# Late additions on VectorE, row copies one key step behind their norms, routing exponentials within slots as powers by GpSimd, and late weight fills spread

## The chip, the cores and the metric

The kernel runs on one core of a Trainium2 chip. The core has five engines with a queue each: TensorE (PE, with its weight loads shown as PEld), VectorE (DVE), ScalarE (ACT), GpSimd (POOL) and SyncE (SP), which here only issues transfers. Each engine takes its own instructions in order, and an instruction that waits holds everything behind it on that engine. The metric is the device time of one execution in microseconds (us), and less is better.

## The reference

Two layers, each an attention over a graph of 2708 nodes with 256 features, and then a mixture of eight experts with two experts for each node:

```python
# layer 0
x = x + elu(softmax(where(adj > 0, q @ k.T / 16, -9e15)) @ v)       # q, k, v of layernorm(x)
x = x + experts0(layernorm(x))      # layernorm again, router, top 2 of 8, gelu(xe @ W1 + b1) @ W2 + b2, hidden 1024
# layer 1
x = x + softmax(where(adj > 0, s_src + s_dst, -1e9)) @ H            # H = layernorm(x) @ W_fc
x = x + experts1(layernorm(x))      # softmax over 8, top 2 of 8, the same with hidden 512
```

The weight of a chosen expert is a softmax: in layer 0 over the two best router values, in layer 1 over all eight. Everything is float32; `adj` is int32.

## The kernel before

The 2708 rows are 22 tiles of 128 rows (the last has 20). Layer-0 attention goes over six blocks of queries (five of 512 and one of 148). A block goes over the 22 tiles of keys, one *key step* each: scores on TensorE, the exponential on ScalarE (L596), the mask on VectorE (L599), and, three key steps later, the product with the values (L648). The scores have two PSUM buffers, so TensorE can be at most two key steps ahead of ScalarE's exponential.

When a block is done, its result tiles are finished and *routed* beside the next block's key steps. This is a chain of small steps for each tile, written as Python generators (`finish`, then `route`). A class `Line` keeps the running chains; each `line.step()` moves every running chain to its next `yield`, oldest first, and starts a new one after every `gap` steps. In layer-0 attention there is one `line.step()` for a key step; in the expert stages there are two for a slot. A chain in layer 0 is: the ELU (L656 to L664), the addition of x (L669 or L671), statistics (L280 to L282), the power for the norm on GpSimd (L286), the normed row (L290), the second copy of the row on ScalarE (L1480), router values, the two best, the exponential on ScalarE (L1525), a count by matmul (L1528, L1529), the weights and the destination (L1531 to L1543), and two indirect transfers from GpSimd that scatter the row to its two experts (L1546). Tiles 0 to 15 get their router values by products on VectorE, tiles 16 to 21 by a transpose and a matmul. In layer 1 tiles 17 to 21 are still in the chain when the expert stage begins; they reach L1525 within it.

An expert stage goes over *slots*: 128 rows for one expert. A slot transposes the gathered rows (L1803), multiplies up (L1830), applies Gelu on ScalarE (L1838, after the scaled bias at L1823), multiplies down (L1846, one slot behind), weights the result on VectorE (L1852) and scatters it from GpSimd (L1868 in layer 0, L1858 in layer 1). GpSimd also fetches the weights of a later slot (L1736) and pads the experts' row lists (L1565), once the last tile is routed. SP fetches rows of later slots (L1755, L1761). The weights lie in a ring of SBUF buffers. In layer 1 the ring has eight buffers; four are filled before the stage (L1729), and four by ScalarE's own transfers in the first slots (L1881, `fill`), two in slot 0 and one each in slots 1 and 2.

The order of TensorE, ScalarE and VectorE is the order in which the program is written (`manual_schedule`), from block 1 of layer-0 attention on through the expert stage, and again in layer 1; SP's order is written out throughout. GpSimd's order in these stages is left to the framework's scheduler.

Of the kernel before, what the change touches and what calls it, by code (L numbers as in the profile page):

```python
# [9 lines left out]
F32 = mybir.dt.float32  # L10
# [5 lines left out]
AF = mybir.ActivationFunctionType  # L16
ALU = mybir.AluOpType
AX = mybir.AxisListType
PSUM = bass.MemoryType.PSUM

P = 128
# [3 lines left out]
E = 8  # L25
# [81 lines left out]
def adj_ffn_kernel(ctx: ExitStack, tc: tile.TileContext, a: dict, out: bass.AP):  # L107
    nc = tc.nc

    const = ctx.enter_context(tc.tile_pool(name="const", bufs=1))  # L110
# [13 lines left out]
    make_identity(nc, ident)  # L124
    minus_half = const.tile([P, 2], F32, name="minus_half")
    nc.gpsimd.memset(minus_half, -0.5)

    minus_big = const.tile([P, P], BF16, name="minus_big")
    nc.vector.tensor_scalar(minus_big, ident, -BIG, None, ALU.mult)
# [137 lines left out]
    def gate_dots(lg, x, r, experts, unused):  # L267

        for e in experts:
            nc.vector.scalar_tensor_tensor(  # L270
                unused, x, 1.0, wr_rows[:r, e],
                op0=ALU.mult, op1=ALU.mult, accum_out=lg[:r, e : e + 1],
            )
# [108 lines left out]
    def layer0_attention(line):  # L382
        with ExitStack() as scope, ExitStack() as until_last:
# [269 lines left out]
            def finish(t, raw, total):  # L653
                r, xr = ROWS[t], xin.pop(t)
                rinv = over_sum(raw, r, D, total, alone[:r, t : t + 1])
                nc.vector.scalar_tensor_tensor(  # L656
                    raw[:r, :D], raw[:r, :D], rinv, bv_b[:r], op0=ALU.mult, op1=ALU.add
                )
                neg = rows0.tile([P, D], F32, name="neg", bufs=2)
                nc.vector.tensor_scalar(neg[:r], raw[:r, :D], 0.0, None, ALU.min)  # L660
                yield
                nc.scalar.activation(neg[:r], neg[:r], AF.Exp)
                yield
                nc.vector.scalar_tensor_tensor(  # L664
                    neg[:r], neg[:r], -1.0, raw[:r, :D], op0=ALU.add, op1=ALU.max
                )
                x1 = rows0.tile([P, D], F32, name="x1")
                if t < experts0.early:
                    nc.vector.tensor_add(x1[:r], neg[:r], xr[:r])  # L669
                else:  # L670
                    nc.gpsimd.tensor_add(x1[:r], neg[:r], xr[:r])  # L671
                    yield
                yield from experts0.route(t, x1)

            def evict(b, accs, total):
# [12 lines left out]
            for b, (b0, nb, ts_) in enumerate(BLOCKS):  # L688
# [14 lines left out]
                for k in range(NT):  # L703
# [15 lines left out]
                    if len(late) > LAG:  # L719
                        b_, k_, p = late.pop(0)  # L720
# [410 lines left out]
    class Experts:  # L1131
        def __init__(self, layer, hidden, packed_weights, gate_bias, own_norm, xd, disp, early):
            self.hidden, self.packed_weights, self.own_norm = hidden, packed_weights, own_norm
            self.gate_bias, self.xd, self.disp = gate_bias, xd, disp

            self.seen = const.tile([P, E], BF16, name=f"seen{layer}")
            nc.vector.memset(self.seen, 0.0)
            self.routed, self.begun, self.pads = 0, False, []
            self.written = []
            self.groups = [f"written{layer}", f"late{layer}", f"apart{layer}", f"after{layer}", f"rows{layer}", f"summed{layer}"]  # L1140
            self.early = early
            self.side = "right" if own_norm else "left"


            n = FULL_AFTER[early]
            self.often = SURE + (2 if own_norm else 4)
            self.ring_size = RING if own_norm else E
            self.rows_ahead = ROWS_AHEAD if own_norm else ROWS_AHEAD + 1
            self.all_slots = SLOTS if own_norm else n + SLOTS
            self.then = {}  # L1150
            if not own_norm:
                self.sum_behind = self.often - E - 1
                return

            size = -(-(SURE - n) // RING)
            runs = [(0, 0, n // RING, 1), (n, size - 1, size, -1)]
            self.number = const.tile([P, SLOTS, 2], F32, name=f"number{layer}")
            number_i = const.tile([P, SLOTS], I32, name=f"number_i{layer}")
            for s0, c0, size, step in runs:
                nc.gpsimd.iota(  # L1160
                    number_i[:, s0 : s0 + size * RING], pattern=[[step, size], [size, RING]],
                    base=c0, channel_multiplier=0,
                )
            s0 = n + size * RING
            nc.gpsimd.iota(
                number_i[:, s0:], pattern=[[1, SLOTS - s0]], base=s0 - n, channel_multiplier=0
            )
            nc.vector.tensor_copy(self.number[:, :, 0], number_i)
            nc.vector.tensor_scalar(
                self.number[:, :, 1], self.number[:, :, 0], float(P), None, ALU.mult  # L1170
            )
# [266 lines left out]
        def route(self, t, x, logits=None):  # L1438


            own_norm, xd, disp, seen = self.own_norm, self.xd, self.disp, self.seen
            gate_bias = self.gate_bias
            r = ROWS[t]
# [4 lines left out]
            mean, once, twice, _ = norm_stats(x[:r], r)  # L1448
# [28 lines left out]
            if own_norm:  # L1477
                if by_dots:
                    gate_dots(dots, x[:r], r, range(E // 2, E), rows2[:r, 1, :D])
                nc.scalar.copy(rows2[:r, 1, :D], rows2[:r, 0, :D])  # L1480
            yield
            if not own_norm:
                (nc.vector.tensor_copy if self.begun else nc.scalar.copy)(
                    rows2[:r, 1, :D], rows2[:r, 0, :D]
# [25 lines left out]
            k = 2 if own_norm else E  # L1510
            p = small.tile([P, E], F32, name="p")
            den = small.tile([P, 2], F32, name="den")
# [9 lines left out]
                nc.vector.memset(sel, 0.0)  # L1522
            nc.vector.tensor_add(sel[:r], hot[:r, 0], hot[:r, 1])
            yield
            nc.scalar.activation(p[:r, :k], p[:r, :k], AF.Exp, accum_out=den[:r, 0:1])  # L1525
            yield
            ps = misc.tile([P, GROUP, P], F32, name="misc").rearrange("p g n -> p (g n)")
            nc.tensor.matmul(ps[:, :E], before, sel, start=True, stop=False)  # L1528
            nc.tensor.matmul(ps[:, :E], ones, seen, start=False, stop=True)  # L1529
# [263 lines left out]
        def slots(self, two, ps_mm, ps_acc, line):  # L1793
            hidden, own_norm, xd = self.hidden, self.own_norm, self.xd
# [82 lines left out]
            n = FULL_AFTER[self.early]  # L1877

            line.gap = 1 if own_norm else 2
            def fill(e):  # L1880
                nc.scalar.dma_start(  # L1881
                    self.ring[e], self.packed_weights[0][e * P : (e + 1) * P, :]
                )
# [4 lines left out]
            def slot(s, s1):  # L1888
                nonlocal placed, placing, behind, xe
                w, (_, who) = self.weights[s], self.rows_[s]  # L1890
                for _ in range(1 + (s == 0)):
                    if fills:
                        fill(fills.pop(0))
                after = turned(1) if s == 0 and not own_norm else None
                hT, bias2 = up(w, xe, who[:, 1:2])
                if s + 1 < s1:
                    xe = after or turned(s + 1)
                line.step()

                def fetch():  # L1900

                    for _ in range(2 if s + AHEAD < n else E):
                        if self.pads:
                            self.pads.pop(0)()
                    if len(self.weights) <= s + AHEAD < often:
                        self.weights.append(self.fetch_weights(s + AHEAD))
                    for _ in range(2):
                        at = len(self.rows_)
                        if at <= s + self.rows_ahead and at < (often if placed else n):
                            while at >= n and self.pads:  # L1910
                                self.pads.pop(0)()
                            self.rows_.append(self.fetch_rows(at))

                if own_norm and not placed and (not line.busy() or s + AHEAD == n):

                    line.finish()
                    for _ in self.place(n, SLOTS):
                        pass
                    placed = True
                if not own_norm and not placed and (not line.busy() or s + AHEAD == n):  # L1920
                    line.finish()
                    if placing is None:
                        placing = self.place_grid(n, self.all_slots)
                    for _ in range(2 if s + AHEAD < n else n):
                        if next(placing, self) is self:
                            placed = True
                            break
                if behind is None:
                    fetch()
                else:  # L1930
                    down(*behind, fetch)
                line.step()
                behind = (s, w, who, hT, bias2)
                if s % 2 == 1 and background:
                    background.pop(0)()
                for start in self.then.get(s, ()):
                    start()
# [177 lines left out]
```

## Time and profile before

| | us |
|---|---|
| median of three runs | 1181.54 |
| range of the runs | 1181.01 to 1186.1 |
| the profiled execution, own time | 1186.52 |
| its span, first to last instruction | 1184.7 |
| TensorE busy | 1134.8 |
| VectorE, ScalarE, GpSimd busy | 645.0, 431.0, 422.4 |
| mean granted TensorE clock | 0.979 |

The profile is of one execution, with times in us from the first instruction. The page gives busy time by engine, then the span in 40 slices; further views list the instructions in order of time (start, duration, engine, line, operation, output<-input, and in brackets how long the engine sat idle before and what ended that), groups of instructions by line and shape (count, busy time, mean in ns, idle before), and busy time with granted clock in chosen stretches. A "granted clock" under 1 means that TensorE was throttled for part of the stretch. Layer-0 attention lasts to about 495, the layer-0 experts to 816, layer-1 attention to 987, and the layer-1 experts to the end.

### The profile page before, as it was taken

How to read it: one execution, taken by the hardware profiler on the slowest of the kernel's cores; microseconds unless marked ns; L12 is line 12 of the kernel's file. 1: busy time of each engine (PE TensorE's matmuls, PEld its weight loads, DVE VectorE, ACT ScalarE, POOL GpSimd, SP SyncE). 2: the span in 40 equal slices, each digit the busy share in tenths (PEclk: the TensorE clock that was granted, in tenths of full speed). 3: DMA queues.
4: the chain of work that ended last, by engine and by line, in shares of the span. 5: the costliest groups of instructions: out<-in, count | busy, mean ns of one | idle time of the engine just before them, and what ended most of it. 6: DMA issues, size and time to landing. Idle time of an engine off the chain costs nothing. (4 is left out here: it accounts for less than half of the span.)

```text
span 1184.7 us, 20877 instructions
## 1 busy us (share of the span) xinstructions
PE 1134.8 (96%) x6421; PEld 919.7 (78%) x6421; DVE 645.0 (54%) x2391; ACT 431.0 (36%) x1258; POOL 422.4 (36%) x517
## 2 busy tenths in 40 slices
PE   8989999999999999899999999998999998999993
PEld 5666666666666675599999999997899997898993
DVE  5555687786887867544222222222876777732224
ACT  3222222222222222253333333332676664744441
POOL 3001212121212123244333343332663554665552
PEclk9999999999999999799999999999999998999997
DMA  9677775867855567548755955552200516577346
GB/s 219 130 163 189 187 183 143 241 165 186 224 129 163 140 154 302 178 125 292 197 155 154 325 128 138 162 161 58 63 1 28 210 51 207 148 241 237 79 119 239
DMA packets 198661, 195.88 MB, mean 165 GB/s; under 512 B 90939, under 2 KB 181524, under 8 KB 192520
## 3 DMA queue, kind: packets, MB, share of 16 engines
q1 hardware_dynamic: 173242, 118.18, 39.1%
q0 software_dynamic: 24256, 70.81, 18.8%
q10 hardware_dynamic: 1038, 5.40, 1.3%
q8 instruction: 55, 0.90, 0.3%
q14 instruction: 70, 0.57, 0.2%
HBM read 246.19 MB, written 66.15 MB: 264 GB/s over the span
## 5 line engine op out<-in xcount | busy, mean ns | idle before, releaser
L1830 PEld LDWEIGHTS mm<-xe,ring 128*128 128x128 f32 x2192 | 261.7, 194 | 9.6 <-ACT raw L678 1.8
L1830 PE MATMUL mm<-xe,ring 128*128 128x128 f32 x2192 | 263.9, 278 | 2.0 <-DVE xe L1803 1.0
L1846 PE MATMUL acc<-ring,hT 128*128 128x256 f32 x1096 | 253.8, 382 | 4.4 <-ACT hT L1838 4.4
L1838 ACT ACTIVATE hT<-mm,ring 128x128 f32<-128x128 f32 x548 | 155.7, 368 | 262.5 <-issue 151.0
L1846 PEld LDWEIGHTS acc<-ring,hT 128*128 128x128 f32 x1096 | 202.5, 191 | 29.1 <-ACT hT L1838 5.1
L648 PEld LDWEIGHTS acc<-v,p 128*128 128x128 f32 (+1 forms) x880 | 160.0, 190 | 62.4 <-issue 36.9
L648 PE MATMUL acc<-v,p 128*128 128x257 f32 (+1 forms) x880 | 202.7, 383 | 0.0
L584 PE MATMUL s<-g,xnT 128*128 128x512 f32 x420 | 201.2, 600 | 0.6 <-DVE mT L603 0.6
L1852 DVE SCALAR_TENSOR_TENSOR y<-acc,who,bias 128x256 f32<-128x256 f32 x92 | 44.4, 483 | 266.1 <-PE acc L1846 246.5
L1546 POOL DMA_INDIRECT disp<-row,to x88 | 91.2, 1037 | 270.6 <-DVE x L669 122.9
L286 POOL TENSOR_TENSOR ln_rs<-ln_rs,minus_half 128x2 f32<-128x2 f32 x88 | 68.8, 783 | 168.1 <-DVE ln_rs L282 126.3
L932 PE MATMUL acc<-parts,m 128*128 128x266 f32 x924 | 126.2, 293 | 0.0
L932 PEld LDWEIGHTS acc<-parts,m 128*128 128x128 f32 x924 | 117.0, 185 | 4.1 <-ACT raw L959 0.9
L1736 POOL DMA_INDIRECT ring<-L_ffn_packed,weight_row x76 | 80.2, 1055 | 111.9 <-PE acc L1846 76.3
L584 PEld LDWEIGHTS s<-g,xnT 128*128 128x128 f32 x420 | 77.2, 191 | 55.1 <-issue 49.5
L596 ACT ACTIVATE p<-s 128x512 f32<-128x512 f32 x105 | 62.3, 596 | 138.8 <-PE s L584 122.6
L599 DVE SCALAR_TENSOR_TENSOR p<-p,mT 128x512 f32<-128x512 f32 x100 | 70.9, 709 | 72.5 <-ACT p L596 72.4
L1868 POOL DMA_INDIRECT xd<-y,who x45 | 71.4, 1587 | 90.3 <-DVE xe L1809 47.3
L899 ACT CAST m<-mT 128x512 fp32r<-128x512 fp8e4 (+4 forms) x168 | 71.9, 475 | 9.6 <-PE acc L932 6.1
L1858 POOL DMA_INDIRECT xd<-y,who x47 | 49.6, 1055 | 51.1 <-DVE y L1852 42.1
L270 DVE SCALAR_TENSOR_TENSOR row<-x,wr_rows 128x256 f32<-128x256 f32 x128 | 54.4, 425 | 3.3
L1809 DVE TENSOR_SCALAR xe<-xe_raw,ring 128x128 f32<-128x128 f32 x90 | 27.3, 352 | 35.7 <-DMA ring<-L_ffn_packed,weight_row 33.7
(336 smaller groups left out, 1094.8 us busy)
## 6 DMA issues: line engine op xcount, KB each, us to landing
adj<-in_adj_dram SPq DMA_DIRECT2D x100, 256.0 KB
L_ffn_packed<-in_L_ffn_W_dram SPq DMA_DIRECT2D x32, 512.0 KB
xg<-disp SPq DMA_DIRECT2D x368, 32.0 KB
L_ffn_packed<-in_L_ffn_W_dram SPq DMA_DIRECT2D x32, 256.0 KB
neighbours<-mT SPq DMA_DIRECT2D x5, 1408.0 KB
mT<-neighbours SPq DMA_DIRECT2D x5, 1408.0 KB
ring<-L_ffn_packed SPq DMA_DIRECT2D x3, 2182.0 KB
xin<-in_x_dram SPq DMA_DIRECT2D x42, 128.0 KB
```

The source lines that it names most:

```text
L286: nc.gpsimd.tensor_tensor(rs[:r, 1], rs[:r, 0], minus_half[:r], ALU.pow)
L584: nc.tensor.matmul(ps[:kr, :nb], xnT[:, c, k0 : k0 + kr], g[:, c, :nb], start=(c == 0), stop=(c == DC - 1 and k < KEYS),)
L599: nc.vector.scalar_tensor_tensor(p, p, LARGEST, mask, op0=ALU.min, op1=ALU.mult)
L648: nc.tensor.matmul(accs[j][:r], p[keys, q0 : q0 + r], v[keys, k, :], start=(k == 0), stop=(k == NT - 1),)
L899: nc.scalar.copy(m[:, : q1 - q0], MASKS[b].of_key(mTs[b], k)[:, q0 - b * BN : q1 - b * BN],)
L932: nc.tensor.matmul(acc[:r], masks[t], parts[:, k, i], start=(k == 0 and i == 0), stop=False,)
L1546: nc.gpsimd.indirect_dma_start(disp[:], bass.IndirectOffsetOnAxis(ap=to[:r, j : j + 1], axis=0), rows2[:r, j], None,)
L1736: nc.gpsimd.indirect_dma_start(w, None, packed[:], bass.IndirectOffsetOnAxis(ap=self.weight_row[:, s : s + 1], axis=0), bounds_check=E * P ...
L1830: nc.tensor.matmul(ps[:, i, :], w[:, c * hidden + f * P : c * hidden + (f + 1) * P], xe[:, c, :], start=(c == 0), stop=(c == DC - 1),)
L1838: nc.scalar.activation(hT[:, f, :], ps[:, i, :], AF.Gelu, bias=w[:, b1 + f : b1 + f + 1])
L1846: nc.tensor.matmul(ps, hT[:, f, :], w[:, w2 + f * D : w2 + (f + 1) * D], start=(f == 0), stop=(f == hc - 1),)
L1868: start = nc.gpsimd.indirect_dma_start(xd[:], at, y, None, bounds_check=N - 1, oob_is_err=False, compute_op=ALU.add)
```

## The change

Five edits:

- x is added to the ELU on VectorE for all tiles; tiles 16 to 21 had it on GpSimd, with a `yield` behind it, which goes too. So everything behind it in these tiles' chains comes one step earlier.
- In layer 0 the second copy of the row on ScalarE comes one step later than the normed row it copies.
- Within the expert stages (flag `slots_run`) the exponential of routing is no longer an activation with an accumulated sum on ScalarE. GpSimd raises a constant tile of 2.71828 to the values by a `tensor_tensor` power over 128x8, and VectorE sums in the next step.
- The four late fills of the ring in layer 1 go 2, 0, 1, 1 in slots 0 to 3; they went 2, 1, 1.
- A constant tile `euler` is set at the start.

```diff
     nc.gpsimd.memset(minus_half, -0.5)
+    euler = const.tile([P, E], F32, name="euler")
+    nc.gpsimd.memset(euler, 2.718281828459045)
...
                 x1 = rows0.tile([P, D], F32, name="x1")
-                if t < experts0.early:
-                    nc.vector.tensor_add(x1[:r], neg[:r], xr[:r])
-                else:
-                    nc.gpsimd.tensor_add(x1[:r], neg[:r], xr[:r])
-                    yield
+                nc.vector.tensor_add(x1[:r], neg[:r], xr[:r])
                 yield from experts0.route(t, x1)
...
             self.routed, self.begun, self.pads = 0, False, []
+            self.slots_run = False
...
                     gate_dots(dots, x[:r], r, range(E // 2, E), rows2[:r, 1, :D])
+            yield
+            if own_norm:
                 nc.scalar.copy(rows2[:r, 1, :D], rows2[:r, 0, :D])
-            yield
...
-            nc.scalar.activation(p[:r, :k], p[:r, :k], AF.Exp, accum_out=den[:r, 0:1])
-            yield
+            if self.slots_run:
+                nc.gpsimd.tensor_tensor(p[:r], euler[:r], p[:r], ALU.pow)
+            else:
+                nc.scalar.activation(p[:r, :k], p[:r, :k], AF.Exp, accum_out=den[:r, 0:1])
+            yield
+            if self.slots_run:
+                nc.vector.tensor_reduce(den[:r, 0:1], p[:r, :k], AX.X, ALU.add)
...
             line.gap = 1 if own_norm else 2
+            self.slots_run = True
...
-                for _ in range(1 + (s == 0)):
-                    if fills:
-                        fill(fills.pop(0))
+                for _ in range((2, 0, 1, 1)[s] if s < 4 and fills else 0):
+                    fill(fills.pop(0))
```

## The prediction

> **What bounds the kernel now.** The page first: TensorE is busy for 1134.8 of 1184.7 us, so a change pays only where TensorE stands still, or runs at a lower clock. The timeline of TensorE, read for its idle brackets, shows no wait above 0.15 us from 127 to 474, nor from 496 to 821 (the layer-0 slots follow each other at 7.03 us). Two places are left that the change touches. The first is the end of layer-0 attention:
>
> ```profile
> 474.12 0.77 PE L584 MATMUL s<-g_last,xnT 128*128 128x148 f32 x4 [2.02 <-ACT p_last L596]
> ...
> 484.24 0.63 PE L617 MATMUL s<-g_last,x_tail 128*32 128x128 f32 x6 [2.04 <-ACT p_last L596]
> ```
>
> Twice TensorE waits 2 us for ScalarE's exponential. ScalarE, VectorE and GpSimd just before the first wait:
>
> ```profile
> 473.47 0.41 ACT L1480 COPY row<-row 128x256 f32<-128x256 f32 x1 [4.80 <-issue]
> 473.78 0.29 ACT L596 ACTIVATE p_last<-s 128x148 f32<-128x148 f32 x1
> ...
> 467.77 1.01 POOL L1546 DMA_INDIRECT disp<-row,to  x1 [0.62 <-ACT p_last L596]
> 469.09 0.97 POOL L1546 DMA_INDIRECT disp<-row,to  x1 [0.30 <-DMA xg<-disp]
> 470.08 0.74 POOL L671 TENSOR_TENSOR x<-neg,xin 128x256 f32<-128x256 f32 x1
> 470.98 1.05 POOL L1736 DMA_INDIRECT ring<-L_ffn_packed,weight_row  x1 [0.16 <-issue]
> 472.06 0.89 POOL L286 TENSOR_TENSOR ln_rs<-ln_rs,minus_half 128x2 f32<-128x2 f32 x1
> ...
> 470.85 0.43 DVE L280 BATCH_NORM_STATS2 ln_st<-x 128x6 f32<-128x256 f32 x1 [2.30 <-POOL x L671]
> 472.98 0.41 DVE L290 TENSOR_SCALAR row<-x,ln_mv,ln_rs 128x256 f32<-128x256 f32 x1 [0.62 <-POOL ln_rs L286]
> ```
>
> Read upward: the exponential stands behind the row copy, which waits for the normed row, which waits for the power, which stands behind the addition, which stands behind two scatters. The second wait is the same chain (copy at 483.59 after 4.97 idle). And behind it the clock falls. Busy time and clock by stretch (PE, PEld, DVE, ACT, POOL, then PEclk):
>
> ```profile
> 484.40:501.60 17.20, 16.23 (x60) 9.85 (x59) 8.90 (x39) 3.06 (x8) 2.03 (x2) 0.52 0.61 201
> 501.60:816.00 314.40, 314.40 (x2150) 295.58 (x2150) 89.66 (x280) 111.59 (x376) 122.21 (x97) 1.00 0.62 177
> ```
>
> The second place is the start of the layer-1 slots: slots 0 to 7 take 37.4 us (987.84 to 1025.26), where eight times 1.78 up and seven times 1.73 down would be 26.4. The 11.1 lost are a wait of 4.45, half clock after it, and ScalarE:
>
> ```profile
> 999.89 3.78 PE L1846 MATMUL acc<-ring,hT 128*128 128x256 f32 x8 [4.45 <-ACT hT L1838]
> ...
> 1004.33 0.33 ACTq L1881 DMA_DIRECT2D ring<-L_ffn_packed  x1
> ...
> 1010.77 1.28 ACT L1525 ACT_TABLE_LOAD   x1
> 1012.07 0.21 ACT L1525 ACTIVATE p<-p 128x8 f32<-128x8 f32 x1
> ...
> 1012.78 1.28 ACT L1838 ACT_TABLE_LOAD   x1
> ```
>
> ScalarE idles from 994.0 to 997.22 and from 1000.6 to 1004.33, and each time a fill is what runs next, so the fill was what waited. Then each routed tile costs two table loads, and ScalarE needs 4.46 a slot against TensorE's 3.51. But GpSimd has no pause from 1009.6 to 1058 beyond the 0.30 behind each indirect transfer, and rows for slot 20 come late:
>
> ```profile
> 1065.53 0.45 DVE L1803 STREAM_TRANSPOSE xe<-xg 128x256 f32<-128x256 f32 x1 [0.58 <-DMA xg<-disp]
> ```
>
> Slot 20's matmul starts at 1067.42, so TensorE is only 1.4 us behind its rows there, and the chain of waits runs back from slot 27 (1093.15, TensorE waiting) through row fetches and result scatters to GpSimd's queue at 1048.
>
> **The change part by part.** *Late additions (six).* They leave GpSimd (0.74 each, 4.5 in all) for VectorE at 0.425 (its row L669), 2.6 us in all in stretches where VectorE has room (25.8 of 37.4 us busy from 447 to 484). The wait of 2.30 for x goes, and with the lost yield the power is issued a key step earlier and the scatters stand a step ahead of it: the power at about 470.1 instead of 472.06, the normed row done at 471.3 instead of 473.4. What is late next is that power, still behind 2.6 us of scatters.
>
> *Row copies (22).* Same 0.41 each, a key step later (1.7 to 1.9 us in the last block), so ScalarE reaches one at about 470.5, waits under 1 us, and has put the exponential before it. In blocks 1 to 4 ScalarE waits up to 6.7 us at these copies, but two score buffers and the lag of three key steps hide it: TensorE has no wait there; I count nothing. Between a copy and its scatter lie three steps or more.
>
> Together: 2.02 + 2.04 of waits, and the clock. The 16.23 us of TensorE work at clock 0.52 would take 8.4, so 7.8 more. [...] I go by the trace: 4.06 + 7.8 = 11.9 us; by the rule 4.1 to 5.8. The layer-0 slots behind it have no wait, so all of it reaches the end of layer 0.
>
> *Exponentials in slots.* Layer 0: up to three tiles, beside slots of 7.03 that wait for nothing; two of the ELU's own exponentials keep their table loads. Nothing; if the cover were gone, 2.6 for each table pair. Layer 1: five tiles lose 2 x 1.28 + 0.4 on ScalarE each, and GpSimd gains five powers over 128x8, VectorE five sums (0.17). No such power is in the trace; the nearest rows:
>
> ```profile
> L286 POOL TENSOR_TENSOR ln_rs<-ln_rs,minus_half 128x2 f32<-128x2 f32 x84 | 65.9, 785 | 167.1 <-DVE ln_rs L282 126.3 <-DVE ln_mv L281 24.5 <-DVE mT L450 12.6
> ...
> L1468 POOL COPY row<-token 128x2 int32<-128x2 int32 x21 | 3.9, 187 | 7.9 <-DVE den L1531 4.2 <-DVE row L290 3.2 <-DVE z L946 0.5
> ```
>
> If all of the power is fixed cost: 0.8. If the 785 - 187 = 598 ns are for two elements, eight cost 0.19 + 8 x 0.30 = 2.6. [...] I take the middle, 1.7.
>
> GpSimd from 989.64 (first scatter) to the first pad (1026.76): 12 scatters x 1.30 + 6 result scatters x 1.30 + 4 powers x 0.74 + 4 copies x 0.2 = 27.2 of work in 37.1. With five powers of 1.7 it is 35.7: if it never waited, the pads would begin 1.4 earlier; at 0.8, 5.9 earlier; at 2.6, 3.1 later. Some waiting remains.
>
> *Fills.* Slot 1 has none, so its Gelu no longer stands behind one: the 4.45 and the half clock (6.8 us at 0.54, 3.1 lost) go. Slots 2 and 3 have one each, and a fill there may again hold ScalarE until a row fetch lands: 0 to 4 us each, I take 2. The two fills of slot 0, which delay the rows, stay.
>
> So TensorE could win some 7 of 11 in this stage, but behind slot 7 it can use only 1.4 more than GpSimd wins: between -6 and +6 for the stage, I take 0.
>
> Sum: 1186.5 - 11.9 + 0 = **1174.6**. The sum is against the profiled execution, which is 5.0 above the median; without the clock drop I expect runs to lie together there, 6.9 (0.6%) under the median. A measurement of this kernel can tell about 0.5% from no change: 1175.6 and 1187.4.
>
> **The rivals.** *Layer 1 wins or loses by GpSimd's pace.* With the power at 0.8 and few waits: 1174.6 - 6 = 1168.7. At 2.6, it is +3 to +6: 1178 to 1181. Nothing in the trace decides between them.
>
> *The clock drop isn't the stall's.* Its tail matmuls use 20 and 32 columns, and that may keep the clock down: only 4.1 is won, 1182.4. [...] Against: 447 to 484 has the same mix at 0.99.
>
> *GpSimd's queue takes ScalarE's place (slower).* A power is issued behind two scatters, and VectorE waits for it in order. In the last block that keeps the normed row more than one step late: copy, waits and half clock stay (0 won). In layer 1, if the power of a tile stands behind the scatters of the tile before, its sum holds VectorE ahead of the next transpose, and a tile goes round in 2.6 (scatters) + 2.6 (power) + 2.9 (VectorE from sum to destination) = 8.1. Before, destinations came from 995.9 to 1022.2, four rounds of 6.6. 4 x 1.5 = 6, so 1192.5. It decides from a power of about 1.1 behind scatters. Against: GpSimd's order isn't the program's (a weight fetch stands before the power at 472.06), and the power's input is ready before the destination.
>
> **How the numbers follow.** Layer 0 in full with layer 1 from -6 to +1: 0.48, below 1175.6. Layer 0 in full with layer 1 worse: 0.17; the clock drop stays: 0.16; both lie within 0.5%. The slower rival: 0.19. Range 1165 (layer 1 at -6 and some luck) to 1188, which leaves out most of the slower rival.
>
> **What would show it.** Right: no TensorE wait near 474 and 484, clock 1.00 from 484 to 502, first layer-0 slot near 486 to 487. No L1525 table loads in slots; two short holds at L1881 in slots 2 and 3. The first pad's start tells GpSimd's share. Wrong: a DVE sum waiting for POOL by over 1 us, or powers over 2.6.

## The result, and the profile after

The changed kernel takes 1179.12 us (median, 1175.60 to 1182.31) against 1182.39 (1179.47 to 1187.82) for the kernel before in the same comparison: a ratio of 0.9968, interval 0.9953 to 0.9983. It is faster by 3.3 us, a little under half of the 6.9 that the forecast put between the medians, and its median is 4.5 over the forecast time of 1174.6. The profiled execution of the changed kernel took 1177.48 (span 1175.8, mean clock 0.99), 9.04 under that of before.

TensorE's timeline after, its larger waits between 200 and 811 us (start, duration, engine, line; in brackets the idle time and what ended it):

```profile
265.06 1.12 PE L570 MATMUL misc<-xnT,aT 128*128 128x512 f32 x2 [0.78 <-ACT g L574]
344.48 1.98 PE L570 MATMUL misc<-xnT,aT 128*128 128x512 f32 x4 [0.78 <-ACT g L574]
...
484.83 1.42 PE L1835 MATMUL mm<-xe,ring 128*128 128x128 f32 x10 [1.07 <-DVE xe L1814]
521.07 0.17 PE L1534 MATMUL misc<-seen,ones 128*128 128x8 bf16 x1 [1.04 <-DVE seen L1542]
```

The two waits of 2 us are gone. Three others have come that the forecast does not have: at the query matmuls of two blocks (0.78 each), and 1.04 at a counts matmul inside the layer-0 slots. The three engines ahead of the place where the first 2.02 stood:

```profile
469.42 0.41 ACT L1481 COPY row<-row 128x256 f32<-128x256 f32 x1 [2.80 <-issue]
469.73 0.29 ACT L598 ACTIVATE p_last<-s 128x148 f32<-128x148 f32 x1
...
466.69 0.42 DVE L670 TENSOR_TENSOR x<-neg,xin 128x256 f32<-128x256 f32 x1
468.92 0.41 DVE L292 TENSOR_SCALAR row<-x,ln_mv,ln_rs 128x256 f32<-128x256 f32 x1 [0.65 <-POOL ln_rs L288]
...
467.16 0.97 POOL L1551 DMA_INDIRECT disp<-row,to  x1 [0.30 <-issue]
468.16 0.72 POOL L288 TENSOR_TENSOR ln_rs<-ln_rs,minus_half 128x2 f32<-128x2 f32 x1
```

The addition is VectorE's, the power follows the two scatters directly, and no weight fetch stands between any more. ScalarE still idles at the copy, 2.80 instead of 4.80, but TensorE does not feel it. By stretch (PE, PEld, DVE, ACT, POOL busy, then PEclk):

```profile
474.20:484.80 10.60, 9.56 (x52) 4.73 (x53) 6.03 (x29) 2.16 (x9) 6.31 (x9) 1.00 0.46 138
484.80:490.10 5.30, 5.27 (x32) 5.29 (x33) 3.20 (x14) 2.43 (x5) 0.00 (x0) 0.68 0.90 371
490.10:811.00 320.90, 318.58 (x2165) 298.29 (x2162) 93.33 (x291) 108.69 (x366) 126.22 (x100) 1.00 0.63 177
```

Instead of 17 us at half clock there is one stretch of 3.4, under the first slot's matmuls (0.68 is its mean with full clock). In the third line TensorE is idle for 2.3 us; before, the line of that stage shows none.

The powers and their sums by shape (four of the five powers over 128 rows, and the sums over eight columns, lie in the layer-1 slots), then from these slots ScalarE at the last fill, two counts matmuls and the longest wait of a sum:

```profile
L1526 POOL TENSOR_TENSOR p<-euler,p 128x8 f32<-128x8 f32 x5 | 8.4, 1676 | 1.2 <-DVE hot L1516 1.1
L1531 DVE TENSOR_REDUCE den<-p 128x1 f32<-128x8 f32 x4 | 0.6, 155 | 4.8 <-POOL p L1526 4.8
...
994.08 0.51 ACT L1828 ACTIVATE bias<-ring,who 128x256 f32<-128x256 f32 x1 [5.88 <-DMA xg<-disp]
...
987.87 0.18 PE L1533 MATMUL misc<-sel,before 128*128 128x8 bf16 x1 [1.63 <-DVE sel L1523]
993.35 0.17 PE L1533 MATMUL misc<-sel,before 128*128 128x8 bf16 x1 [1.25 <-DVE sel L1523]
...
1007.75 0.15 DVE L1531 TENSOR_REDUCE den<-p 20x1 f32<-20x8 f32 x1 [2.54 <-POOL p L1526]
```

A power over 128x8 takes 1.68 us, and sums wait for it up to 2.54. The fill still holds ScalarE (5.88), but the wait of 4.45 for the Gelu is gone; shorter waits for VectorE have taken its place (1.63, 1.25, 0.73, 0.31 and 0.75), and 3.4 us at half clock are left (from 994.57). Slots 0 to 7 take 35.7 us, after 37.4.

A table of stages helps to read all that follows. Each entry is the difference of two starts on TensorE in one profiled execution: attention from the first score matmul of block 1 (126.96 in before, 122.99 after) to the first slot; the layer-0 slots to the first matmul behind them (L992, L990 after); layer-1 attention to its first slot; the layer-1 slots to the end of the span. "Half" is the time at half clock inside the first two stages.

| kernel (run) | attention 0 | slots 0 | half | attention 1 | slots 1 |
|---|---|---|---|---|---|
| before | 368.8 | 325.3 | 17.1 | 166.8 | 196.8 |
| powers alone (2) | 366.1 | 324.7 | 3.4 | 166.4 | 199.1 |
| fills alone (3) | 366.1 | 324.1 | 10.2 | 165.9 | 199.7 |
| additions alone (5) | 362.1 | 326.9 | 3.4 | 166.9 | 200.1 |
| copies alone (6) | 367.9 | 325.5 | 10.2 | 165.6 | 198.1 |
| changed | 361.8 | 326.4 | 3.4 | 165.7 | 198.8 |
| changed, run again (12) | 361.9 | 324.5 | 0 | 165.1 | 201.1 |
| layer 0 alone, mended (13) | 360.1 | 324.6 | 3.4 | 165.6 | 201.1 |
| changed, yield kept (14) | 362.2 | 324.5 | 3.4 | 165.7 | 197.7 |
| changed, early copies back (15) | 359.8 | 325.9 | 0 | 166.4 | 196.7 |
| changed, both mended (16) | 360.1 | 323.3 | 0 | 165.4 | 197.7 |

The remaining 4.0 of the difference between the two profiled executions lies ahead of all this: before had 6.8 us at half clock from 84.5 on, the changed kernel none. Run again, the same changed kernel had them too and started attention at 126.78. So this part comes and goes with one kernel, and I don't count it to the change.

### The profile page after: what moved, and what is told of

Read it like the earlier page. It is cut to its first block, busy times and chain, and to the rows that moved or that the text cites. A ratio compares the mean times of both kernels' runs of the same rounds, so it can differ in the third digit from the quotient of the medians.

```text
span 1175.8 us, 20858 instructions
## 1 busy us (share of the span) xinstructions
PE 1125.0 (96%) x6421; PEld 912.2 (78%) x6421; DVE 647.7 (55%) x2405; ACT 415.4 (35%) x1232; POOL 430.3 (37%) x519
```

## The experiments

Each ratio is to the kernel before, measured on the same chip. Its median there was 1184.07 for runs 1 to 4, 1181.77 for 5 to 8, 1183.96 for 9 to 12 and 1184.47 for 13 to 16. The profile of a run is of one execution, and not always a typical one.

### 1 to 4: the parts

**1, late additions and row copies alone.**

```
-if t < experts0.early: vector.tensor_add ... else: gpsimd.tensor_add ...; yield
+nc.vector.tensor_add(x1[:r], neg[:r], xr[:r])
 ...
-                nc.scalar.copy(rows2[:r, 1, :D], rows2[:r, 0, :D])   # ahead of the yield
+                nc.scalar.copy(rows2[:r, 1, :D], rows2[:r, 0, :D])   # behind it
```

> Only the late additions on VectorE and the row copies a key step later; exponentials and fills as before. Theory (the gain lies at the end of layer-0 attention, and what the slots get back or lose is small): about all of the change's gain, 3 to 5 us under the kernel before. Rival (the layer-1 slots give away some of it, by the powers or the spread fills): this kernel is then faster than the changed one by about 2 us, 5 to 7 us under before. Rival (the two waits are worth only their 4.06 us less what the new copies make TensorE wait, twice 0.78): 2 to 3 us under before.

1181.05 us, ratio 0.9975 (0.9963 to 0.9987): 3.0 under before. The waits of 2 us are gone, the ones of 0.78, 0.78 and 1.04 are there: those three belong to this part, not to the powers. Theory and the second rival both allow 3.0; the sum of the waits (4.06 - 1.56 - 1.04 = 1.5) allows half of it.

**2, powers alone.** Only the `if self.slots_run:` branches and `euler`.

> Only the exponentials of the slots as powers on GpSimd; the rest as before. Theory (a power stands in GpSimd's queue between scatters, and the sum holds VectorE): 1 to 3 us slower than before, with sums that wait 1 to 2.5 us for a power and the first pad within 1 us of 38.9 us behind the stage's begin. Rival (the table loads saved on ScalarE are worth more): 1 to 3 us faster, TensorE waiting less for the Gelu in slots 0 to 7.

1183.51 us, ratio 1.0003 (0.9984 to 1.0021): no difference that this measurement shows, so neither figure. What this run tells most about is layer 0, which is that of before:

```profile
470.65 0.77 PE L586 MATMUL s<-g_last,xnT 128*128 128x148 f32 x4 [2.02 <-ACT p_last L598]
...
480.76 0.41 PE L619 MATMUL s<-g_last,x_tail 128*32 128x128 f32 x6 [2.03 <-ACT p_last L598]
...
489.60 1.61 PE L1838 MATMUL mm<-xe,ring 128*128 128x128 f32 x8 [3.03 <-DMA xg<-disp]
```

The same two waits, and no half clock up to the first slot. But the first slot now waits 3.03 for its rows. In layer 1 three of the sums wait 1.6 to 2.5 us for a power, as expected.

**3, fills alone.**

```
-for _ in range(1 + (s == 0)): if fills: fill(fills.pop(0))
+for _ in range((2, 0, 1, 1)[s] if s < 4 and fills else 0): fill(fills.pop(0))
```

> Only the weight fills spread (two in slot 0, none in slot 1, one each in slots 2 and 3); the rest as before. Theory (a hold moves from slot 1 to slots 2 and 3 and is worth the same): within 1 us of before, TensorE's 4.45 us wait for the Gelu replaced by two shorter ones. Rival (the half clock behind the wait goes and is worth its 3 us): 2 to 3 us faster.

1181.57 us, ratio 0.9984 (0.9966 to 1.0003), which leaves both open by the time. In the trace the wait for the Gelu moved from slot 1 (4.45) to slot 3 (4.18): the theory's picture. Layer 0 is again that of before, and here 6.8 us of half clock lie behind the first 2-us wait:

```profile
471.90:478.70 6.80, 6.67 (x20) 4.12 (x20) 3.59 (x20) 1.04 (x6) 4.20 (x7) 0.50 0.21 68
...
489.33 2.05 PE L1830 MATMUL mm<-xe,ring 128*128 128x128 f32 x8 [2.18 <-DMA xg<-disp]
```

Attention takes 366.12 here and 366.11 in run 2. Half clock cost nothing in the end: no second wait of 2 us follows here (TensorE came later to that place), and the wait for the first rows is 2.18 instead of 3.03.

**4, all but the powers.** Runs 1 and 3 together.

> The change without the powers: the exponentials of the slots stay on ScalarE. Theory (powers cost 1 to 3 us in the layer-1 slots): 1 to 3 us faster than the changed kernel, so 4 to 6 us under before. Rival (powers pay for themselves by the table loads): 1 to 3 us slower than the changed kernel, 0 to 2 us under before.

1178.67 us, ratio 0.9957 (0.9941 to 0.9972), beside 0.9968 (0.9953 to 0.9983) with the powers. The intervals overlap; a cost of the powers of 1 to 3 us is not shown.

### 5 to 8: inside the layer-0 part

**5, additions alone** (the first hunk of run 1).

> Only the six late additions go to VectorE, with the yield behind them gone; row copies, exponentials and fills as before. Theory (the additions alone bring the normed row early enough for the exponential, and their lost yield makes two tiles' counts meet): the waits of 2.0 us at the last block's score matmuls are gone or under 0.5 us, no wait of 0.78 at the query matmuls of blocks 2 and 3, the wait of 1.04 us at a counts matmul in the layer-0 slots is there; 3 to 4 us under before. Rival (the row copy's place decides): both waits of 2.0 us stay within 0.5 us, and the time is within 1 us of before.

1182.12 us, ratio 0.9985 (0.9968 to 1.0002). The waits are 1.55 and 0.39 instead of 2.0 each, the first slot waits 1.13, the 1.04 is there, no 0.78: the additions alone do less than the theory said, and the 1.04 is theirs. Attention still falls to 362.1, so they bring 4.0 of the 6.0 that all of the mended layer-0 part brings (360.1).

**6, copies alone** (the second hunk).

> Only the row copies of layer 0 come a key step later; the late additions stay on GpSimd. Theory (additions and copies are both needed, and the copies cost twice 0.78 us at the query matmuls): the two 2.0-us waits stay at 1 us or more each, two new waits of 0.78 us, within 1.5 us of before. Rival (the copy's place alone decides): both 2.0-us waits gone, 2 to 3 us under before.

1186.79 us, ratio 1.0037 (1.0018 to 1.0055): slower by 5.0 at the median. The theory was wrong on the waits, the rival on the time:

```profile
474.40 0.61 PE L1495 MATMUL misc<-wr,raw 128*128 128x8 f32 x4 [2.43 <-ACT raw L304]
...
491.06 1.20 PE L1831 MATMUL mm<-xe,ring 128*128 128x128 f32 x4 [3.22 <-DVE xe L1810]
```

No score matmul waits any more, so the place of the copy alone ends both 2-us waits. Then a gate matmul waits 2.43 and the first slot 3.22: with the addition still on GpSimd everything behind it is late, and the wait only moves on. Both edits are needed, for different waits. The two of 0.78 are there, so they are the copies'. How the whole 5.0 comes about is not shown: the profile is of this kernel's fastest execution (1182.05), and its attention takes only 1.8 more than in runs 2 and 3.

**7, late copies only, without the powers.** As run 4, but for the early tiles the copy stays ahead of the yield:

```
 if own_norm: ...
+    if t < self.early: nc.scalar.copy(...)      # as before
 yield
+if own_norm and t >= self.early: nc.scalar.copy(...)
```

> Late additions on VectorE without their yield, row copies a key step later for the late tiles alone (the early tiles' copies stay where they were), fills spread, exponentials on ScalarE. Theory (moving the early copies is what makes the query matmuls wait twice 0.78): those waits are gone, and the time is 1 to 2 us under the kernel with all copies moved, so 6 to 7 us under before. Rival (the early copies are worth nothing either way, the 0.78 has another cause): same as that kernel, 5 us under before.

1177.37 us, ratio 0.9958 (0.9936 to 0.9980). The waits of 0.78 are gone and attention takes 359.8: the theory holds for the waits. The time is 4.4 under before, short of the 6 to 7 expected and not separable from run 4.

**8, the yield kept.** As run 7, with `yield` left behind the late addition.

> As the kernel before it in this list, but with the yield behind the late additions kept. Theory (the lost yield lets two tiles' counts meet in one slot): the 1.04-us wait at the counts matmul in the layer-0 slots is gone, and the normed rows of the last block come a key step later without a wait over 0.5 us at the score matmuls: 7 to 8 us under before. Rival (without the lost yield the rows are late again): one or both waits of 2 us come back in part, 3 to 5 us under before.

1175.90 us, ratio 0.9932 (0.9907 to 0.9956). The 1.04 is gone, no score matmul waits, the largest wait of TensorE from 130 us up to the first slot is 0.57. The theory holds for the waits; in time, 5.9 under before by the medians, the interval reaches from 5 to 11 us and overlaps that of run 7.

### 9 to 12: layer 1

**9, four fills in slot 0.** Run 8 with `(4, 0, 0, 0)`.

> Late additions on VectorE with the yield kept, late row copies a key step later, exponentials on ScalarE, and all four weight fills in slot 0 of layer 1. Theory (a fill holds ScalarE only because it stands behind row fetches that wait for routed rows, and slot 0's are issued before those): no hold of ScalarE over 1.5 us in slots 1 to 5, the TensorE wait of 4 to 5 us at slot 4 gone; 2 to 4 us under the same kernel with the fills in slots 0, 2 and 3, so 9 to 12 us under before. Rival (four fills at once delay the first rows by their own traffic): the first slots' transposes wait for rows 2 to 5 us longer, and the time is the same as or over the kernel with the fills spread.

1180.58 us, ratio 0.9979 (0.9963 to 0.9994); run 8 has 0.9932. The theory fell:

```profile
972.55 15.04 ACTq L1884 DMA_DIRECT2D ring<-L_ffn_packed  x4
987.64 0.51 ACT L1826 ACTIVATE bias<-ring,who 128x256 f32<-128x256 f32 x1 [14.78 <-DMA xg<-disp]
```

Issued in a row, the fills hold ScalarE for 14.8 us, until a row fetch has landed, and TensorE waits 11.57 for the Gelu. Two fills in slot 0 are not held (0.83 us for both in before and in the changed kernel); four in a row are, and so is every fill in slots 1 to 3 of before (ScalarE idle for 3.65 and 4.15 us), of the changed kernel (3.79 and 5.88) and of run 8 (1.80 and 5.27). In the traces of before and of the changed kernel the fills and SyncE's row fetches use the same eight semaphores (101 to 108), and each held fill of the two starts 0.02 to 0.03 us behind the last landing of a row fetch on its semaphore. In before the fill at 997.22 waits for 102, which a row fetch issued at 991.72 had taken and whose last landing is at 997.20; in the changed kernel the one at 993.71 waits for 101, taken at 987.42, with the last landing at 993.69.

**10, with the powers.** Run 8 plus the powers.

> Late additions on VectorE with the yield kept, late row copies a key step later, fills in slots 0, 2 and 3, and the powers on GpSimd. Theory (powers cost about 1 us more than the table loads that they save): 0 to 2 us over the same kernel with the exponentials on ScalarE, which lay 6 to 10 us under before. Rival (with TensorE earlier at layer 1, GpSimd is the bound and the powers cost their whole queue time): 3 to 6 us over it.

1173.68 us, ratio 0.9918 (0.9895 to 0.9940), against 0.9932 without, on another chip: again no cost of the powers is shown.

**11, short powers.** The changed kernel with `p[:r, :2]` for `p[:r]` in the power and the sum. In layer 1 it so leaves out six of the eight terms of the softmax sum.

> The changed kernel with powers and sums over two columns instead of eight in the slots (in layer 1 the other six terms of the softmax sum are left out). Theory (a power's time goes by its elements: 0.8 us at two columns against 1.7 at eight, and VectorE's sums wait for it): powers at 0.75 to 0.85 us, sums waiting 0.5 to 1 us less each, TensorE's waits on sel and seen in slots 0 to 7 down by 2 us or more, 1 to 3 us under the changed kernel. Rival (the place in GpSimd's queue behind the scatters decides, not the length): the sums still wait 1 to 2.5 us, time within 1 us of the changed kernel.

1176.56 us, ratio 0.9952 (0.9931 to 0.9973); the changed kernel beside it has 0.9964 (run 12), so the time does not decide. The trace does for the power's length, and for the theory:

```profile
L1526 POOL TENSOR_TENSOR p<-euler,p 128x2 f32<-128x2 f32 x5 | 3.8, 752 | 0.8 <-DVE hot L1516 0.8
L1531 DVE TENSOR_REDUCE den<-p 128x1 f32<-128x2 f32 x6 | 0.9, 149 | 1.6 <-POOL p L1526 1.6
```

0.75 us at two columns, 1.68 at eight. Slot 8 begins 32.4 us behind the stage's begin instead of 35.7, the first pad 34.4 instead of 38.7. Yet slot 28 begins at 108.6, against 110.7 in the changed kernel and 108.9 in before. Of the lead over before (5.0 at slot 8) 0.3 is left, of that over the changed kernel (3.3) 2.1. In before, the changed kernel, this run and run 16 the row fetch of slot 20 is issued 20.4 to 21.1 us behind the last pad, and rows come late behind it. SP (SyncE) in the changed kernel shows the pause, 69.9 behind the stage's begin, and VectorE the late rows, for slots 26 and 27:

```profile
1039.10 1.04 SPq L1766 DMA_DIRECT2D who<-disp  x1
1046.82 1.86 SPq L1760 DMA_DIRECT2D xg<-disp  x4
...
1078.50 0.45 DVE L1808 STREAM_TRANSPOSE xe<-xg 128x256 f32<-128x256 f32 x1 [4.55 <-DMA xg<-disp]
1083.51 0.45 DVE L1808 STREAM_TRANSPOSE xe<-xg 128x256 f32<-128x256 f32 x1 [4.20 <-DMA xg<-disp]
```

**12, the changed kernel again.**

> The changed kernel as it is, beside the others on one chip. Theory (its gain is the two waits less what they turn into, and no clock drop of 17 us stands in a usual run of before): 2 to 5 us under before, and another execution has its half-clock stretches at other places, of at most 7 us each ahead of 1158 us. Rival (the long drop is usual in before and the change takes it away): 7 to 12 us under before.

1180.33 us, ratio 0.9964 (0.9948 to 0.9980): the 3.6 under before repeat the 3.3. Half clock lies at 84.4 (6.8 us), 995.8 and 1081.1 (3.4 each), and at the end of the span; in the first profile it lay at 486.0 and 994.6. The theory holds.

### 13 to 16: what layer 0 gave back

**13, layer 0 alone, mended.** Late additions with the yield kept, late copies only; powers and fills as before.

> The layer-0 part alone in its mended form: late additions on VectorE with the yield kept, row copies a key step later for the late tiles alone; exponentials and fills as before. Theory (the 4.06 us of waits are worth 4 us or more once nothing is given back in layer 0): 4 to 7 us under before, against 3.0 for additions and copies as the change has them. Rival (what is won in layer 0 is lost again in layer 1, whose row fetches set its end): 2 to 3 us under before, as the change's own additions and copies.

1176.78 us, ratio 0.9935 (0.9910 to 0.9960): 7.7 under before, where run 1 got 3.0. What layer 0 wins does reach the end.

**14, the changed kernel with the yield kept.**

> The changed kernel with the yield behind the late additions kept, all else as changed. Theory (the lost yield costs the 1.04-us wait and a little more): that wait gone, the two of 0.78 still there, 1 to 2 us under the changed kernel, so 4.5 to 6 us under before. Rival (the copies are the whole give-back): within 0.7 us of the changed kernel.

1176.72 us, ratio 0.9945 (0.9926 to 0.9963). The 1.04 is gone, the two of 0.78 are there, as expected; the interval overlaps that of the changed kernel, so by the time the yield's worth is not shown.

**15, the changed kernel with the early copies back in their place.**

> The changed kernel with the early tiles' row copies put back to their place, all else as changed. Theory (their move costs twice 0.78 us): those waits gone, the 1.04 still there, 1.5 to 2.5 us under the changed kernel, so 5 to 6.5 us under before. Rival (the yield is the whole give-back): within 0.7 us of the changed kernel.

1175.55 us, ratio 0.9918 (0.9887 to 0.9948): 8.9 under before by the medians, more than expected. The waits of 0.78 are gone, the 1.04 is there. There are only six executions, here and in the next run.

**16, both mended.** The kernel of run 10 again.

> Yield kept, early copies in their place, powers and spread fills: the version that lay 9.7 us under before. Theory (both give-backs are separate and add up): 7 to 10 us under before again, and under the two kernels with one of them mended by 1 us or more. Rival (that result was a favourable draw of clock stretches): 4 to 6 us under before, as those two.

1174.70 us, ratio 0.9909 (0.9881 to 0.9937), after 0.9918: this version beats before and the changed kernel, whose interval begins at 0.9948 (run 12). It is not separated from run 15, nor from run 13, so that the two give-backs add up is shown by the waits and stages and not by the time. No wait of 0.78 or 1.04 is left, attention is 360.1 and the layer-0 slots 323.3.

## Why the prediction was right or wrong

**In short.** The forecast of 6.9 between the medians was 4.06 for the two waits and 2.8 for the clock drop (its 7.8 less the 5.0 by which the profiled execution lay over the median), with nothing given back. Three steps of it failed: the price of the clock drop, "I count nothing" for the early row copies, and "all of it reaches the end of layer 0". An estimate from the stage table: the end of the waits is worth 6.0, the copies take back 1.7 to 2.1, the lost yield 0.7 to 2.3. That leaves 1.6 to 3.6; measured are 3.3 and 3.6. So the forecast was too high although the waits brought more than their sum.

**The two waits: right, and worth more than the sum said.** Both went. Attention fell from 366.1 (runs 2 and 3, with the layer 0 of before) to 361.8, although two new waits of 0.78 lie inside it; without those it is 360.1. So their end is worth 6.0, not 4.06: the first slot's wait (2.02 + 2.03 + 3.03 = 7.08 with the two others in run 2) shrinks to 1.07 as well. The profile of before did not show that wait: there TensorE came later, after half clock, and waited only 0.97, for ScalarE.

**"I count nothing" for the early row copies: wrong.** That TensorE had no wait at these copies before was true, and said nothing about the step behind. Moved, they cost twice 0.78 at the query matmuls (there in runs 1, 4, 6, 11, 12 and 14; gone in 7 to 10, 13, 15 and 16), 1.7 to 2.1 in the attention stage. Why the second query group then waits for the first one's evacuation was not found.

**The lost yield: counted only as a gain.** It was to bring the normed row a step earlier, and with the yield kept attention is as short (360.1 beside 359.8). But it also carries the last tiles' routing differently into the slots, where a counts matmul waits 1.04 for `seen`. With the yield kept, the wait is gone. The step "the layer-0 slots behind it have no wait, so all of it reaches the end of layer 0" failed here: in the stage table the layer-0 slots of the changed kernel take 1.2 (run again, no half clock in them) and 3.1 more than those of run 16. Three pairs of profiles differ in the yield alone: runs 7 and 8, 12 and 14, 15 and 16. With half of the half clock taken off (an estimate of what it costs) the stage is longer without the yield by 1.0, 1.7 and 2.6; 0.3 of it comes back in attention. The named wait is 1.04 of this; for the rest no cause was found.

**The clock drop of 7.8: mis-sized, and the largest miss of the sum.** Against runs 2 and 3, before lost 2.7 in attention and about 1 in the slots behind it, not 7.8. Two things were wrong. First, TensorE at full clock would have stood waiting for the first rows, as in run 2 (3.03 us); of the half clock only what outlasts that wait is lost. Second, the drop differs between executions. Of three profiles with that layer 0, one has five windows of half clock (17.1 us, before) from the second wait on, one has two (6.8 us, run 3) behind the first wait, and one has none before the first slot (run 2). In the traces of before and of the changed kernel all half-clock stretches begin at one phase of a period of 3.413 us (before at 84.49, 483.85, 828.60, 999.26 and 1169.93; the changed kernel at 485.98, 994.57 and 1158.41), and that phase differs between the two (2.57 and 1.29 us behind a whole number of periods from the first instruction). The windows at that phase, around the second wait, first in before and then in run 2 (PE, PEld, DVE, ACT, POOL busy, then PEclk):

```profile
480.44:483.85 3.41, 1.76 (x11) 0.74 (x9) 1.47 (x5) 0.26 (x1) 2.71 (x7) 1.00 0.60 154
483.85:487.26 3.41, 3.02 (x14) 1.34 (x14) 1.73 (x10) 1.23 (x6) 0.91 (x1) 0.50 0.90 379
...
476.46:479.87 3.41, 2.27 (x15) 1.25 (x14) 1.30 (x5) 0.00 (x0) 3.19 (x8) 1.00 0.54 136
479.87:483.29 3.42, 2.53 (x19) 1.61 (x20) 1.90 (x12) 1.49 (x6) 0.41 (x1) 1.00 0.82 332
483.29:486.70 3.41, 3.28 (x12) 0.94 (x10) 1.34 (x8) 0.10 (x1) 3.08 (x3) 1.00 0.94 367
```

In before, the window with the wait held 1.76 us of TensorE work and the clock fell behind it; in run 2 the same wait was shared by two windows with 2.27 and 2.53, and it did not. But the busy time of a window alone doesn't decide. A window with 1.90 us (from 470.20 in before) was not followed by half clock. A window with 2.34 that ends at the first slot was followed by it in the changed kernel (from 485.98), and one with the same 2.34 was not when that kernel ran again. What else counts stays open. The trace was right as far as it went: the clock fell at 483.85, within the wait of 2.04, and stayed at half for 17.1 us. The forecast's "by the rule 4.1 to 5.8" was not read from a trace: its 5.8 is the waits and 1.7 for a drop, and no run shows that 1.7. At the same 2-us waits the profiles have 17.1 us at half clock (before), 6.8 (run 3) and none (run 2), and before lost the 2.7 and about 1. With the phase and the length of a drop so different between executions, one execution's drop was not to be priced in full. Over the executions of run 12 the mean clock is 0.9885, against 0.9862 for before on that chip: 0.0023 of 1180 us, an estimate of 2.7 us at the most and if none of it were hidden.

**The power: right, with luck.** Taken 1.7, measured 1.68. But 1.7 was the middle between two guesses, 0.8 and 2.6, and no row of before spoke for it. The line through the two measured lengths (0.75 at two columns, 1.68 at eight) is 0.44 + 0.155 an element, an estimate that no third length tests.

**First pad 1.4 earlier: measured 0.3** (38.9 to 38.65 behind the stage's begin). GpSimd's work was sized right, and the 1.4 was for a GpSimd that never waits: from its first scatter to the first pad it took 36.85 (978.71 to 1015.56), with about 35.6 of work by the same count, so 1.3 of waiting remained of 9.9. (One reading of before was off without effect: GpSimd does pause 1.00 ahead of its scatter at 1023.06.)

**Fills: right in kind.** Holds of 3.79 and 5.88 us of ScalarE in slots 2 and 3 instead of 2 each, the second above the 4 allowed; TensorE was mostly waiting for VectorE by then. The wait of 4.45 went, but of the 7 us that TensorE could win up to slot 7 only 1.7 came.

**Layer 1 at 0, between -6 and +6: not contradicted, but hardly tested.** The stage took 2.0 more in the first pair of profiles, and lies between 196.7 and 204.4 over all profiles, in no order of the edits; in the five kernels with the layer 1 of before it goes from 196.8 to 201.1. That a gain in slots 0 to 7 need not last agrees with the profiles: with slot 8 begun at 35.7 in six of them, slot 28 begins anywhere from 106.8 to 114.2. What makes that spread was not found.

**The rivals.** "A DVE sum waiting for POOL by over 1 us" did come: four of the five sums waited 1.23 to 2.54. So GpSimd's queue did in part take ScalarE's place, but the slower kernel that was to follow did not come (run 2: 1.0003). The rival needed each power behind two scatters. Two of the five stand there, three stand ahead of a pair, as here:

```profile
994.07 1.68 POOL L1526 TENSOR_TENSOR p<-euler,p 128x8 f32<-128x8 f32 x1
995.95 1.04 POOL L1551 DMA_INDIRECT disp<-row,to  x1 [0.20 <-POOL p L1526]
```

The last four rounds of destinations take 5.7 each (986.42 to 1009.17), after 6.6 in before, where the rival had 8.1.

By its time the measured 1179.1 falls into the 1178 to 1181 of the first rival, but by luck, for that was for powers of 2.6. By its gain, "the clock drop isn't the stall's" with 4.1 lies nearest, but for another reason: in the end of attention, ahead of the first slot, half clock came only behind a wait of 2 us or more (2.04 in before, 2.01 in run 3, 2.43 in run 6, of 18 profiles). So here the drop came with the stall, only not always (run 2 had waits of 2.02 and 2.03 and no drop there), and it was mostly hidden (the 2.7 and about 1, of 7.8). The forecast's sign, a first layer-0 slot near 486 to 487, seems met by 484.83; without the 4.0 from the start of the profile it would be 488.8, and run again it is 488.63.

**What the give-backs cost.** With both mended, runs 13 and 16 win 7.7 and 9.8 between the medians, where run 1 and the changed kernel win 3.0 and 3.3 to 3.6. In stages, run 16 against the first profile of the changed kernel: 1.7 in attention, 3.1 in the layer-0 slots (of it up to 1.7 from the half clock at the first slot), 1.2 in layer 1, 0.8 elsewhere. The waits named account for 2.6 of it. How the rest divides between fewer clock drops (mean clock 0.9905 in run 16) and the few executions timed is not settled.

## What to carry to other kernels

A step that is moved for some tiles should be moved for those tiles only: here the same move for the others cost TensorE twice 0.78 us where nothing had waited. When an edit drops a yield, follow the tile past the stage that you are looking at, into the next one. And price a clock drop from several executions, after asking what TensorE would wait for if the clock had been full.

## What the runs showed of the hardware

Half-clock stretches, but for the last of a profile, came in whole multiples of 3.41 us, at one phase per execution (before: 6.83, 17.07, 3.41 and 6.83 us; the changed kernel: 3.41 twice), and a wait of 2 us was followed by five of them (17.1 us, before), two (6.8, run 3) or none (run 2). Once low, the clock in before stayed low through windows in which TensorE was busy for 3.02, 3.42, 3.41 and 2.44 us, with narrow tail matmuls among the first of them. Weight fills issued by ScalarE waited for row fetches issued by SyncE on the same semaphores: in before a fill started at 997.22, behind the landing on semaphore 102 at 997.20, with ScalarE idle for 3.65 us, and with four fills in a row (run 9) ScalarE idled for 14.8 us until a row fetch landed. A `tensor_tensor` power on GpSimd took 0.75 us over 128x2 (run 11) and 1.68 over 128x8 (the changed kernel).
